# Graph attention and masked attention on one core: the product with the values between the next pair's scores

## The chip, the cores and the metric

The kernel runs on one core of a Trainium2 chip. The metric is the device time of one execution in microseconds (us); lower is better. Engines are named as in the profile: PE is TensorE, DVE is VectorE, ACT is ScalarE, POOL is GpSimd, and SP is the engine whose queue issues most transfers.

## The reference, cut to what matters

For each of 32 batches there are 512 rows of 512 numbers. Layer 0 is a graph attention, layer 1 a masked attention with 8 heads of 64; behind each stand a residual and a layer norm.

```python
# layer 0
h = X @ W                                             # 512 -> 256
e = leaky_relu(h @ a[0] + (h @ a[1]).T, 0.2)          # 512 x 512
alpha = softmax(e + NEG * (1 - adj), -1)
x1 = layernorm(x + concat([alpha @ h, h], -1))
# layer 1
q, k, v = (split_heads(x1 @ W.T + b) for W, b in ((Wq, bq), (Wk, bk), (Wv, bv)))
attn = softmax(where(adj == 0, -inf, (q @ k.T) / 8), -1)     # 8 heads of 512 x 512
out = layernorm(x1 + merge_heads(attn @ v) @ Wo.T + bo)
```

Everything is float32.

## The kernel before

All instructions are in program order on every engine: the text of the kernel is a schedule written out by hand, and each engine works through its own part of it without overtaking. The outer loop runs over batches `b`, the inner one over the four pairs of heads `hp`. While batch `b` is in its attention, the output product of batch `b-1` is finished (`finish_seven`, a generator that is advanced piece by piece with `next(seven)`), and layer 0 of `b+1` and the first products of `b+2` are done.

One pair goes like this:

- `head_scores(b, hp, i)`, called for tiles i = 0 to 3: PE makes the scores of 128 rows for both heads into PSUM (tile `ps`, four banks, so two tiles i at a time). DVE adds the mask and takes the maximum (`minus_max`, L315); ACT takes the exponential and its sum (L710) into a tile `p`.
- `head_blocks` (L722): DVE turns each of the eight `p` in blocks of 32 x 32 into the tile `t` (L330, eight instructions), inverts the sums (L717), sends them to memory (`d_tot`, L719), and SP issues 16 transfers of 128 KB from `t` to `pt` (`move_pair`, L347), which finish the transposition. `t` and `pt` have one buffer each: the first transposition of the next pair cannot begin until all 16 transfers of this one have landed.
- `head_inverse` (L750): POOL reads the inverse sums back, broadcast over partitions.
- `head_values` (L753): PE multiplies `pt` with the values (`pav`), and DVE multiplies with the inverse sums (L771).

Two products of PE are spread over the pairs, and their PSUM tiles share four banks with `pav`: `project_two` (queries and keys, `pw`, L547) after pairs 1 and 3, `project_v` (values, `pv`, L623) in pair 0, the output product of the batch before (`pf`, L791) in pairs 1 and 2, layer 0's product with the values (`po`, L477) after pair 1, and its projection (`ph`, L264) in pair 3. Each of `project_two`, `project_v` and `finish_seven` follows a scheme with seven products of half size: a first product goes to a bank, ACT copies it (`p1`), and a later product is accumulated onto the same bank, so that PE cannot go on before ACT has copied.

The order of PE in a batch before the change is, pair by pair (01 and 23 are the score tiles of the pair, and `pav` belongs to the pair before):

```
pair 0:  ps01, pv, ps23, pav, pv
pair 1:  ps01, pf, ps23, pav, po, pw
pair 2:  ps01, pf, ps23, pav, pf
pair 3:  ps01, ph, ps23, pav, pw
```

ACT's order matters too. In pair 1 the root for layer 0's norm (`ln_root` in `l0_output`, L286), which needs the statistics that DVE takes from all four `po`, stands ahead of the copies of `pw` (L571). In pair 3 the root for the norm of the finished batch (`ln_root`, after `out_stats`) stands ahead of the exponentials of tiles 2 and 3, and `out_norm` (L902) between these and the copies of `pw`.

Of the kernel before, what the change touches and what calls it, by code (L numbers as in the profile page):

```python
# [14 lines left out]
P = 128  # L15
# [11 lines left out]
def kernel(  # L27
# [47 lines left out]
    nc = tc.nc  # L75
    B, N, F = x.shape
# [65 lines left out]
            nc.sync.dma_start(xt_sb, src)  # L142
        st["xt", b] = xt_sb

    def load_x(b):
        x_sb = io.tile([P, NB, F], F32, name=f"x_{b}", tag="x", bufs=3)
        nc.sync.dma_start(x_sb, x[b].rearrange("(c p) f -> p c f", p=P))
        st["x1", b] = x_sb


# [175 lines left out]
    def transpose_blocks(t, i, src):  # L326

        nc.vector.transpose(  # L330
            t[:, :, :, i, :].rearrange("p r c q -> p c r q"),
            src.rearrange("p (c r k) -> p c r k", r=4, k=G),
        )
# [9 lines left out]
    def move_pair(dst, t):  # L343

        for g in range(4):
            for r in range(4):
                nc.sync.dma_start(  # L347
                    dst[r * G : (r + 1) * G, g], t[g * G : (g + 1) * G, r]
                )
# [119 lines left out]
            nc.vector.tensor_tensor(et[:, j, :], et[:, j, :], row, ALU.subtract)  # L469
            nc.scalar.activation(et[:, j, :], et[:, j, :], AF.Exp)  # L470

    def l0_values(b, i):
        h_sb, z = st["h", b], st["x1", b]
        et = st["et", b]
        po = (psum_s if b == 0 else psum)(f"po_{b}_{i}")[:, : F1 + 1]
        for j in range(NB):
            nc.tensor.matmul(  # L477
                po,
                et[:, j, i * P : (i + 1) * P],
                h_sb[:, j, 2:],  # L480
                start=(j == 0),
                stop=(j == NB - 1),
            )
        inv = small.tile([P, 1], F32, name=f"inv0_{b}_{i}", tag="inv0", bufs=2)
        nc.vector.reciprocal(inv, po[:, F1:])
        nc.vector.scalar_tensor_tensor(
            z[:, i, :F1], po[:, :F1], inv, z[:, i, :F1], ALU.mult, ALU.add
        )
# [126 lines left out]
    def project_v(b):  # L615

        x1t, tx = st["x1t", b], st["tx", b]
        half = F // 2

        def product(ps, columns, weights, start=True):  # L620
            for k in range(2):
                for c in range(FC // 2):
                    nc.tensor.matmul(  # L623
                        ps[:, k * half : (k + 1) * half],
                        columns(k, c),
                        weights(c),
                        start=start and k == 0 and c == 0,
                        stop=c == FC // 2 - 1,
                        skip_group_check=True,
                    )  # L630

        def a_(i, f):
            cols = slice(i * half, (i + 1) * half)
            return lambda c: wv_sb[:, 2 * f + c, cols]

        def s_(i):
            return lambda c: wvx_sb[:, i, c, :]

        def b_(f, j):
            return lambda k, c: x1t[:, 2 * j + k, 2 * f + c, :]  # L640

        def t_(i):
            return lambda k, c: tx[:, i, k, c, :]

        def copy(ps, name):
            t = prob.tile([P, N], F32, name=f"{name}_{b}_v", tag="p", bufs=PB)
            nc.scalar.copy(t, ps)
            return t

        out = []  # L650
        for j in range(2):
            v = act.tile([P, 2, F], F32, name=f"v_{b}_{j}", tag="v", bufs=2)
            st["v", b, j] = v
            out.append(v)

        def result(i, j, ps, other):
            nc.vector.tensor_tensor(
                out[j][:, :, i * half : (i + 1) * half],
                ps.rearrange("p (k d) -> p k d", k=2),
                other.rearrange("p (k d) -> p k d", k=2),  # L660
                ALU.add,
            )

        b1 = psum(f"pv1_{b}")
        product(b1, b_(0, 0), a_(0, 0))
        p1 = copy(b1, "p1")
        yield
        b3, b4 = psum(f"pv3_{b}"), psum(f"pv4_{b}")
        product(b3, t_(0), s_(0))
        p5 = copy(b3, "p5")  # L670
        product(b4, t_(2), a_(1, 0))
        p7 = copy(b4, "p7")
        nc.gpsimd.tensor_tensor(p7, p7, p5, ALU.add)
        product(b1, t_(1), s_(1), start=False)
        u2 = copy(b1, "u2")
        b2 = psum(f"pv2_{b}")
        product(b2, b_(1, 0), a_(0, 1))
        product(b3, b_(1, 1), s_(2), start=False)
        product(b4, t_(3), a_(1, 1), start=False)
        yield  # L680
        result(0, 0, b2, p1)
        result(0, 1, b3, u2)
        result(1, 1, b1, p7)
        result(1, 0, b4, u2)

    def head_scores(b, hp, i):
# [18 lines left out]
        for j in range(2):  # L705
# [6 lines left out]
            )  # L712
            st.setdefault(("p", b, hp), []).append((j, i, p))

    def head_sums(b, hp):
        total = st.pop(("tot", b, hp))
        nc.vector.reciprocal(total, total)  # L717
        d = dram.tile([2, P, NB], F32, name=f"d_tot_{b}_{hp}", tag="dtot")
        nc.sync.dma_start(d.rearrange("j p i -> p j i"), total)  # L719
        st["inv", b, hp] = d  # L720

    def head_blocks(b, hp):  # L722
        t = st.pop(("t", b, hp))
        for j, i, p in st.pop(("p", b, hp)):
            transpose_blocks(t[:, :, j], i, p)
        head_sums(b, hp)
        pt = prob.tile([P, 4, 2, FC, NB, G], F32, name=f"pt_{b}_{hp}", tag="pt", bufs=1)
        move_pair(pt, t)
        st["pt", b, hp] = pt

    def head_turn(b, hp):

        pt = prob.tile([P, 4, 2, FC, NB, G], F32, name=f"pt_{b}_{hp}", tag="pt", bufs=1)
        for k, (j, i, p) in enumerate(st.pop(("p", b, hp))):
            ps = psum_s(f"pt_{b}_{hp}_{i}_{j}")
            for c in range(FC):
                cols = slice(c * P, (c + 1) * P)
                nc.tensor.transpose(ps[:, cols], p[:, cols], ident)  # L738
            (nc.vector.tensor_copy if k % 2 == 0 else nc.scalar.copy)(
                pt[:, :, j, :, i, :].rearrange("p g c q -> p c g q"),  # L740
                ps.rearrange("p (c g q) -> p c g q", c=FC, g=4),
            )
        head_sums(b, hp)
        st["pt", b, hp] = pt

# [4 lines left out]
            nc.gpsimd.dma_start(inv[j * D : (j + 1) * D], d[j].partition_broadcast(D))  # L750
        st["inv", b, hp] = inv

    def head_values(b, hp, bank=None):  # L753
        pt, inv = st.pop(("pt", b, hp)), st.pop(("inv", b, hp))
        po = (bank or psum)(f"pav_{b}_{hp}")
        for c in range(NB):
            for j in range(2):
                head = 2 * hp + j
                nc.tensor.matmul(  # L759
                    po[j * D : (j + 1) * D, :],  # L760
                    st["v", b, c // 2][:, c % 2, head * D : (head + 1) * D],
                    pt[:, :, j, c, :, :].rearrange("p g i q -> p g (i q)"),
                    start=(c == 0),
                    stop=(c == NB - 1),
                )
        if hp % 2 == 0:
            st["ot", b, hp // 2] = act.tile(
                [P, 2, N], F32, name=f"ot_{b}_{hp // 2}", tag="ot", bufs=3
            )
        ot = st["ot", b, hp // 2][:, hp % 2]  # L770
        nc.vector.tensor_tensor(  # L771
            ot.rearrange("p (g i q) -> p g i q", g=4, i=NB),
            po.rearrange("p (g i q) -> p g i q", g=4, i=NB),
            inv.rearrange("p (g q) i -> p g i q", g=4),
            ALU.mult,
        )

    def finish_seven(b):


        z = st["x1", b]
# [44 lines left out]
        to = prob.tile([P, 2, N], F32, name=f"to_{b}", tag="rows", bufs=1)  # L826
        t1, t2, t3, t4 = b12, b22, to[:, :, : 2 * P], b21
        nc.gpsimd.tensor_tensor(t3, b22, b12, ALU.subtract)
        nc.gpsimd.tensor_tensor(t1, b12, b11, ALU.subtract)
        nc.gpsimd.tensor_tensor(t2, b22, t1, ALU.subtract)  # L830
        nc.gpsimd.tensor_tensor(t4, t2, b21, ALU.subtract)
# [4 lines left out]
        add(nc.vector, 0, 0, b1)  # L836
        yield
        b4, b5 = psum(f"pf4_{b}"), psum(f"pf5_{b}")
        product(b1, t2, s_(1), start=False)
        u2 = copy(b1, "u2")  # L840
        product(b4, t3, a_(1, 0))
        p7 = copy(b4, "p7")
        add(nc.gpsimd, 0, 1, u2)
        add(nc.gpsimd, 1, 0, u2)
        yield
        product(b5, t1, s_(0))
        product(b4, t4, a_(1, 1), start=False)
        yield
        add(nc.vector, 1, 1, b5)
# [125 lines left out]
    def output_bias():  # L975
# [4 lines left out]
        )  # L980
        nc.vector.tensor_tensor(bo_sb, pb, bo_sb, ALU.add)

    before = None
    turned = {(0, 2), (B - 2, 2), (B - 1, 2), (B - 1, 3)}
    for b in range(B):
        more = b < B - 1
        seven = finish_seven(b - 1) if b > 0 else None
        for hp in range(NP):
# [44 lines left out]
                out_norm(b - 1)  # L1033
            if (b, hp) not in turned:
                head_blocks(b, hp)
            if hp == 0 and b > 0 and more:
                load_x(b + 1)
            if before is not None:
# [45 lines left out]
            else:  # L1084
# [14 lines left out]
                head_inverse(b, 3)  # L1099
                if b == 0:  # L1100
                    weight_negative(OUTPUT)
                    add_bias(1)
            before = (b, hp)
    b = B - 1
    ln_root(f"1_{b - 1}")
# [72 lines left out]
```

## Time and profile before

| what | value |
|---|---|
| median of 3 runs | 3072.32 us (3070.25 to 3075.42) |
| profiled execution | 3078.44 us, span 3076.7 us |
| PE busy | 3044.9 us, 99% of the span |
| DVE busy | 2493.5 us, 81% |
| ACT busy | 1536.4 us, 50% |
| POOL busy | 1254.5 us, 41% |
| transfers `pt<-t` | 1984 of 128 KB, issued by SP |

Busy time is what an engine's instructions took; the chain is the work that ended last, followed back to its start. A line such as L330 is a line of the kernel before. In a timeline the columns are the start, the duration (from the start of the first to the end of the last of merged instructions), the engine, the line, the operation, output and inputs, and a count; square brackets give the engine's idle time ahead of it and what ended it.

### The profile page before, as it was taken

What the parts mean: (1) busy time and instruction counts of PE and PEld (TensorE: products, weight loads), DVE (VectorE), ACT (ScalarE), POOL (GpSimd) and SP (SyncE); (2) the same over time, 40 slices, a digit from 0 to 9 for tenths busy, and PEclk for the clock granted to TensorE, in tenths of its full rate; (3) what the DMA queues carried; (4) which work ended last, traced back from release to release, by engine and by line L of the source; (5) the groups of instructions that cost most, each with busy time, mean ns of one, the idle gap of its engine ahead of it and who ended that gap; (6) DMA issues with size and microseconds to landing.
All of it is one profiled execution on the core that took longest, in us unless ns stands there. A gap on an engine that the chain in (4) does not pass through costs nothing.

```text
span 3076.7 us, 44833 instructions
## 1 busy us (share of the span) xinstructions
PE 3044.9 (99%) x13492; PEld 2064.9 (67%) x13492; DVE 2493.5 (81%) x5707; ACT 1536.4 (50%) x3264; POOL 1254.5 (41%) x1224
## 2 busy tenths in 40 slices
PE   8999999999999999999999999999999999999999
PEld 6666666666666666666666666666666666666665
DVE  7788788888888888888888888878888877888765
ACT  4445554545544455544455444555454554445544
POOL 4343444444344434344443444343444434443422
PEclk9999999999999999999999999999999999999999
DMA  6456665566566656655665656566556656666642
GB/s 185 113 134 155 153 159 146 150 162 165 145 156 150 161 154 154 162 146 147 163 163 145 154 151 163 154 151 163 149 146 162 164 144 157 151 160 155 155 102 66
DMA packets 244865, 462.54 MB, mean 150 GB/s; under 512 B 94544, under 2 KB 97104, under 8 KB 244624
## 3 DMA queue, kind: packets, MB, share of 16 engines
q1 hardware_dynamic: 232160, 425.83, 54.9%
q0 software_dynamic: 12464, 33.84, 4.2%
q8 instruction: 109, 1.79, 0.3%
q14 instruction: 132, 1.08, 0.1%
HBM read 132.65 MB, written 34.27 MB: 54 GB/s over the span
## 4 chain that ended last, share of the span: by engine, by line
PE 90%; DVE 3%; SPq 2%; issue 1%; POOL 1%; DMA 1%; ACT 1%; DVEq 0%; ACTq 0%; POOLq 0%
PE pw L547 23%; PE ps L701 14%; PE pav L759 14%; PE pv L623 12%; PE pf L791 12%; PE po L477 7%; PE ph L264 7%; SPq L347 2%; DVE t L330 1%; DMA d_least<-least 1%; DVE p L315 1%; PE pf L863 0%; PE pt L738 0%; DVE junk L315 0%; DMA adjs_sb<-in_adj_dram 0%
## 5 line engine op out<-in xcount | busy, mean ns | idle before, releaser
L710 ACT ACTIVATE p<-p,least 128x512 f32<-128x512 f32 x1024 | 725.8, 711 | 518.5 <-DVE least L315 315.6
L315 DVE CUSTOM_DVE_ANT_0 p<-ps,mask 128x512 f32<-128x512 f32 x1024 | 645.0, 686 | 224.0 <-PE ps L701 223.9
L330 DVE STREAM_TRANSPOSE t<-p 128x512 f32<-128x512 f32 x992 | 603.0, 675 | 8.7 <-issue 6.5
L701 PE MATMUL ps<-qk 64*128 64x512 f32 x2048 | 512.5, 617 | 4.1 <-DVE qk L584 3.8
L759 PE MATMUL pav<-pt,v 128*64 128x512 f32 x2048 | 467.7, 598 | 7.7 <-DMA pt<-t 4.0
L759 PEld LDWEIGHTS pav<-pt,v 128*64 128x64 f32 x2048 | 138.9, 136 | 322.0 <-issue 283.0
L701 PEld LDWEIGHTS ps<-qk 64*128 64x128 f32 x2048 | 179.2, 186 | 210.7 <-issue 163.6
L459 POOL TENSOR_TENSOR et<-et,mask0t 128x512 f32<-128x512 f32 x126 | 144.4, 1159 | 341.6 <-ACT et L455 341.4
L750 POOL DMA_DIRECT2D inv<-d_tot x256 | 134.4, 530 | 276.9 <-DMA d_tot<-tot 92.8
L814 POOL TENSOR_TENSOR x<-x,u_o 128x512 f32<-128x512 f32 x93 | 117.0, 1272 | 306.8 <-ACT u_o L809 275.4
L477 PE MATMUL po<-h,et 128*128 128x257 f32 x1024 | 233.9, 387 | 2.8 <-ACT et L470 2.2
L264 PE MATMUL ph<-w_sb,xt 128*128 128x258 f32 x1024 | 233.4, 385 | 0.3 <-DVE w_sb L190 0.3
L477 PEld LDWEIGHTS po<-h,et 128*128 128x128 f32 x1024 | 190.4, 191 | 58.9 <-POOL x L379 25.3
L264 PEld LDWEIGHTS ph<-w_sb,xt 128*128 128x128 f32 x1024 | 192.2, 190 | 50.8 <-PE ps L701 22.0
L379 POOL TENSOR_TENSOR x<-x,h 128x256 f32<-128x256 f32 x128 | 85.6, 701 | 306.7 <-DMA x<-in_x_dram 306.7
L536 POOL TENSOR_TENSOR x<-x,bo_sb 128x512 f32<-128x512 f32 x128 | 158.5, 1272 | 94.1 <-DVE x1t_b L330 94.1
L710 ACT ACTIVATION_READ_ACCUMULATOR p<-p,least 128x1 f32 x1024 | 192.1, 188 | 0.0
L710 ACT ACT_TABLE_LOAD x62 | 79.5, 1283 | 218.9 <-DVE least L315 218.4
L286 ACT ACTIVATE rstd<-mv,eps 128x4 f32<-128x4 f32 (+1 forms) x66 | 19.6, 297 | 335.3 <-DVE mv L281 331.9
L280 DVE BATCH_NORM_STATS2 stats<-x 128x6 f32<-128x512 f32 x252 | 171.8, 682 | 16.2 <-POOL x L814 3.1
L791 PE MATMUL pf<-wo_sb,ot 128*128 128x256 f32 x744 | 182.2, 388 | 0.0
L791 PE MATMUL pf<-wox_sb,ot 128*128 128x256 f32 x744 | 179.0, 383 | 0.0
(154 smaller groups left out, 5453.0 us busy)
## 6 DMA issues: line engine op xcount, KB each, us to landing
pt<-t SPq DMA_DIRECT2D x1984, 128.0 KB, 3.5
x<-in_x_dram SPq DMA_DIRECT2D x32, 1024.0 KB, 5.4
inv<-d_tot POOLq DMA_DIRECT2D x256, 128.0 KB, 3.9
xt<-in_xt_dram SPq DMA_DIRECT2D x31, 1024.0 KB, 5.6
x1t<-x1t_b SPq DMA_DIRECT2D x496, 64.0 KB, 2.0
out_dram<-x SPq DMA_DIRECT2D x31, 1024.0 KB, 5.7
rows<-d_att SPq DMA_DIRECT2D x31, 512.0 KB, 3.7
rows<-d_least SPq DMA_DIRECT2D x31, 256.0 KB, 3.6
```

Of the source, the lines that this page charges most:

```text
L264: nc.tensor.matmul(ps, lhs(c), rhs(c), start=(c == 0), stop=(c == FC - 1))
L280: nc.vector.bn_stats(stats, z[:, i, :])
L315: nc.vector.tensor_tensor_reduce(out=out, in0=scores, in1=mask, scale=-1.0, scalar=MIN_INIT, op0=ALU.add, op1=ALU.min, accum_out=least,)
L330: nc.vector.transpose(t[:, :, :, i, :].rearrange("p r c q -> p c r q"), src.rearrange("p (c r k) -> p c r k", r=4, k=G),)
L477: nc.tensor.matmul(po, et[:, j, i * P : (i + 1) * P], h_sb[:, j, 2:], start=(j == 0), stop=(j == NB - 1),)
L536: nc.gpsimd.tensor_tensor(z[:, i, :], z[:, i, :], bo_sb, ALU.add)
L547: nc.tensor.matmul(ps[:, k * half : (k + 1) * half], weights(k, c), moving(c), start=start and k == 0 and c == 0, stop=c == FC // 2 - 1, s ...
L623: nc.tensor.matmul(ps[:, k * half : (k + 1) * half], columns(k, c), weights(c), start=start and k == 0 and c == 0, stop=c == FC // 2 - 1, ...
L701: nc.tensor.matmul(ps, qk[rows, 0, i * P : (i + 1) * P], qk[rows, 1, :], start=True, stop=True)
L710: nc.scalar.activation(p, p, AF.Exp, bias=least, scale=-1.0, accum_out=total[:, j, i : i + 1])
L759: nc.tensor.matmul(po[j * D : (j + 1) * D, :], st["v", b, c // 2][:, c % 2, head * D : (head + 1) * D], pt[:, :, j, c, :, :].rearrange("p ...
L791: nc.tensor.matmul(ps[:, k * half : (k + 1) * half], columns[:, c, k * P : (k + 1) * P], weights(c), start=start and k == 0 and c == 0, st ...
```

## The change

For batches 1 to 29 a new function `middle_batch` writes out the order of a batch; batches 0, 30 and 31 keep the old loop. In the middle batches:

- In pairs 0, 1 and 2 the product `pav` of the pair before (`head_products`) is issued between score tiles 01 and 23; in pair 3 it stays behind tile 3. The division by the sums (`head_divide`) stays behind the pair's transpositions.
- Four of the eight transpositions of a pair are issued after the maxima of tiles 0 and 1 (`head_blocks` is called twice), the other four after tiles 2 and 3. The move to `pt` comes ahead of the write of the inverse sums.
- `project_v` runs wholly after pair 0's scores. The first two pieces of `finish_seven` go to the end of pair 0, and the tile `po` 0 follows them there; the other three `po` stay after pair 1. The four sums on POOL move to the middle of pair 1, the product b1 to the end of pair 2's scores, and the rest stays behind pair 2.
- The load of `x` for the next batch is issued by POOL, between two of these sums, and not by SP.

In all batches `project_v` writes its (1, 1) result first, and `finish_seven` does two products ahead of the accumulation onto b1. `add_bias(1)` moves from the end of batch 0 to batch 1.

```diff
-    def load_x(b):
+    def load_x(b, engine=nc.sync):
...
-        nc.sync.dma_start(x_sb, x[b].rearrange("(c p) f -> p c f", p=P))
+        engine.dma_start(x_sb, x[b].rearrange("(c p) f -> p c f", p=P))
...
     def head_blocks(b, hp):
-        t = st.pop(("t", b, hp))
         for j, i, p in st.pop(("p", b, hp)):
-            transpose_blocks(t[:, :, j], i, p)
-        head_sums(b, hp)
+            transpose_blocks(st["t", b, hp][:, :, j], i, p)
+
+    def head_move(b, hp):
         pt = prob.tile([P, 4, 2, FC, NB, G], F32, name=f"pt_{b}_{hp}", tag="pt", bufs=1)
-        move_pair(pt, t)
+        move_pair(pt, st.pop(("t", b, hp)))
...
         nc.gpsimd.tensor_tensor(t3, b22, b12, ALU.subtract)
+        if between:
+            between()
         nc.gpsimd.tensor_tensor(t1, b12, b11, ALU.subtract)
...
         b4, b5 = psum(f"pf4_{b}"), psum(f"pf5_{b}")
+        product(b4, t3, a_(1, 0))
+        p7 = copy(b4, "p7")
+        product(b5, t1, s_(0))
         product(b1, t2, s_(1), start=False)
         u2 = copy(b1, "u2")
-        product(b4, t3, a_(1, 0))
-        p7 = copy(b4, "p7")
...
+    def pair_ends(b, hp):
+        head_blocks(b, hp)
+        head_reciprocal(b, hp)
+        head_move(b, hp)
+        head_sums(b, hp)
+
+    def middle_batch(b):
+        seven = finish_seven(b - 1, lambda: load_x(b + 1, nc.gpsimd))
+        for hp in range(NP):
+            last = (b, hp - 1) if hp > 0 else (b - 1, NP - 1)
+            head_scores(b, hp, 0)
+            head_scores(b, hp, 1)
+            if hp < 3:
+                head_products(*last)
+            if hp == 0:
+                l0_scores(b + 1, [0, 1])
+            elif hp == 1:
+                next(seven)
+                l0_add_h(b + 1)
+            elif hp == 2:
+                add_bias(b + 1)
+            head_blocks(b, hp)
+            if hp == 3:
+                out_stats(b - 1)
+                for i in range(NB):
+                    l0_project(b + 2, i)
+                l0_columns(b + 2)
+                ln_root(f"1_{b - 1}")
+            head_scores(b, hp, 2)
+            head_scores(b, hp, 3)
+            if hp == 2:
+                next(seven)
+            elif hp == 3:
+                out_norm(b - 1)
+                head_products(*last)
+            pair_ends(b, hp)
+            if hp == 2:
+                next(seven)
+            head_divide(*last)
+            if hp == 0:
+                l0_row(b + 1)
+                l0_scores(b + 1, [2, 3])
+                leaky(st["row", b + 1])
+                values = project_v(b)
+                next(values)
+                next(values)
+                l0_weights(b + 1)
+                head_inverse(b, 0)
+                steps(values)
+                next(seven)
+                next(seven)
+                l0_value_product(b + 1, 0)
+            elif hp == 1:
+                l0_output(b + 1)
+                load_xt(b + 2)
+                two = project_two(b, 1)
+                next(two)
+                l0_norm(b + 1)
+                next(two)
+                head_inverse(b, 1)
+                blocks = x1_blocks(b + 1)
+                for part in (blocks, two, blocks, two, blocks):
+                    next(part, None)
+            elif hp == 2:
+                steps(seven)
+                x1_sums(b + 1, nc.gpsimd)
+                head_inverse(b, 2)
...
+            else:
+                l0_maxima(b + 2)
+                l0_write(b + 2)
+                l0_read(b + 2)
+                store(b - 1)
+                steps(project_two(b + 1, 0))
+                head_inverse(b, 3)
...
     for b in range(B):
+        if 0 < b < B - 2:
+            middle_batch(b)
+            before = (b, NP - 1)
+            continue
```

More of the change, by code (lines that the diff above doesn't have):

```diff
@@ L470, in l0_weights, with l0_value_product @@
             nc.scalar.activation(et[:, j, :], et[:, j, :], AF.Exp)
-    def l0_values(b, i):
-        h_sb, z = st["h", b], st["x1", b]
-        et = st["et", b]
+    def l0_value_product(b, i):
+        h_sb, et = st["h", b], st["et", b]
         po = (psum_s if b == 0 else psum)(f"po_{b}_{i}")[:, : F1 + 1]
@@ L483, in l0_values @@
             )
+        st["po", b, i] = po
+    def l0_values(b, i):
+        z = st["x1", b]
+        if ("po", b, i) not in st:
+            l0_value_product(b, i)
+        po = st.pop(("po", b, i))
         inv = small.tile([P, 1], F32, name=f"inv0_{b}_{i}", tag="inv0", bufs=2)
@@ L680, in project_v @@
         yield
+        result(1, 1, b1, p7)
         result(0, 0, b2, p1)
         result(0, 1, b3, u2)
-        result(1, 1, b1, p7)
         result(1, 0, b4, u2)
@@ L713, in head_scores, with head_reciprocal @@
             st.setdefault(("p", b, hp), []).append((j, i, p))
+    def head_reciprocal(b, hp):
+        total = st["tot", b, hp]
+        nc.vector.reciprocal(total, total)
     def head_sums(b, hp):
         total = st.pop(("tot", b, hp))
-        nc.vector.reciprocal(total, total)
         d = dram.tile([2, P, NB], F32, name=f"d_tot_{b}_{hp}", tag="dtot")
@@ L751, in head_inverse, with head_products @@
         st["inv", b, hp] = inv
-    def head_values(b, hp, bank=None):
-        pt, inv = st.pop(("pt", b, hp)), st.pop(("inv", b, hp))
-        po = (bank or psum)(f"pav_{b}_{hp}")
+    def head_products(b, hp, bank=None):
+        pt = st.pop(("pt", b, hp))
+        po = st["pav", b, hp] = (bank or psum)(f"pav_{b}_{hp}")
         for c in range(NB):
@@ L765, in head_values, with head_divide @@
                 )
+    def head_divide(b, hp):
+        po, inv = st.pop(("pav", b, hp)), st.pop(("inv", b, hp))
         if hp % 2 == 0:
@@ L776, in head_values, with finish_seven @@
         )
-    def finish_seven(b):
+    def head_values(b, hp, bank=None):
+        head_products(b, hp, bank)
+        head_divide(b, hp)
+    def finish_seven(b, between=None):
         z = st["x1", b]
@@ L845, in finish_seven @@
         yield
-        product(b5, t1, s_(0))
         product(b4, t4, a_(1, 1), start=False)
@@ L981, in output_bias @@
         nc.vector.tensor_tensor(bo_sb, pb, bo_sb, ALU.add)
+    def pair_ends(b, hp):
+        head_blocks(b, hp)
+        head_reciprocal(b, hp)
+        head_move(b, hp)
[61 more added lines that the diff above has]
+                head_inverse(b, 2)
+                if b == 1:
+                    add_bias(1)
+            else:
[5 more added lines that the diff above has]
+                head_inverse(b, 3)
@@ L1035 @@
                 head_blocks(b, hp)
+                head_reciprocal(b, hp)
+                head_sums(b, hp)
+                head_move(b, hp)
             if hp == 0 and b > 0 and more:
@@ L1101 @@
                     weight_negative(OUTPUT)
-                    add_bias(1)
             before = (b, hp)
```

## The prediction

> **What bounds the kernel now.** I read the page first: is one engine always at work?
>
> ```profile
> PE 3044.9 (99%) x13492; PEld 2064.9 (67%) x13492; DVE 2493.5 (81%) x5707; ACT 1536.4 (50%) x3264; POOL 1254.5 (41%) x1224
> ...
> pt<-t SPq DMA_DIRECT2D x1984, 128.0 KB, 3.5
> ```
>
> A busy PE might still be a slow PE, so I took one batch by windows:
>
> ```profile
> 1518.00:1612.00 94.00, 94.00 (x419) 63.86 (x418) 77.58 (x178) 47.56 (x101) 39.53 (x38) 1.00 0.62 160
> ```
>
> PE has no gap at all in 94 us and its clock is 1.00. In the timeline eight records of 256 columns that follow their like take 1.725 us; a batch has 416 records of that weight, 89.8 us, and the rest up to the period of 93.83 is spread over 20 switches between full products, `ps` and `pav`: about 0.2 us each. So PE sets the time, at a floor. The waits of PE say where that floor is thin:
>
> ```profile
> PE pav L759 <- DMA pt<-t: 4.0, 2, 2.8
> PE pav L759 <- DMA d_least<-least: 2.7, 6, 1.4
> ```
>
> `pav` is the only product that ever waits in the middle: the one of pair 3, in pair 0 of the next batch. The move to `pt` lands just in time there. On the chain the `pw` of pair 1 starts at 379.27 and, 22 batches on, at 2447.06: 93.99 a batch.
>
> Next, how close the others follow. Pair 1, PE, then ACT:
>
> ```profile
> 1587.94 1.99 PE L701 MATMUL ps<-qk 64*128 64x512 f32 x8
> 1589.85 3.65 PE L759 MATMUL pav<-pt,v 128*64 128x512 f32 x16
> 1593.44 7.25 PE L477 MATMUL po<-h,et 128*128 128x257 f32 x32
> ...
> 1604.84 1.03 PE L547 MATMUL pw<-tx,wk_sb 128*128 128x256 f32 x4
> 1605.84 1.13 PE L547 MATMUL pw<-tx,wqx_sb 128*128 128x256 f32 x4
> ```
>
> ```profile
> 1605.02 0.30 ACT L286 ACTIVATE rstd<-mv,eps 128x4 f32<-128x4 f32 x1 [10.89 <-DVE mv L281]
> 1605.22 1.54 ACT L571 COPY p<-pw 128x512 f32<-128x512 f32 x3
> ```
>
> PE's step from 1604.84 to 1605.84 is 1.00 where its neighbours take 0.86: the accumulation at 1605.84 waited 0.1 us for ACT's copy, which waited for the root, which waited for DVE. There is no slack here at all.
>
> Pair 3, DVE, SP and ACT (`ps` of tiles 2 and 3 begins at 1544.68):
>
> ```profile
> 1548.87 4.86 DVE L330 STREAM_TRANSPOSE t<-p 128x512 f32<-128x512 f32 x8 [0.21 <-issue]
> ```
>
> ```profile
> 1532.67 11.09 SPq L347 DMA_DIRECT2D pt<-t  x16
> ...
> 1554.46 10.51 SPq L347 DMA_DIRECT2D pt<-t  x16
> ```
>
> ```profile
> 1551.16 2.92 ACT L902 ACTIVATE x<-x,shift,rstd 128x512 f32<-128x512 f32 x4
> 1553.98 1.04 ACT L571 COPY p<-pw 128x512 f32<-128x512 f32 x2
> ```
>
> One move keeps SP for 10.0 to 11.1 us and its last transfer lands 2.5 to 3.6 us after its issue, so `t` is taken for 13.1 us from the last transposition on (0.15 + 9.9 + 3.0 without the write of the sums ahead of it). Before, the next transpositions came 16.8 us later.
>
> **The change, part by part.** All times in us; "ps23" is the start of tiles 2 and 3.
>
> *Switches of PE.* With `pav` between `ps01` and `ps23`, and `pv` no longer split, pairs 0, 1 and 2 have four switches, not five: 3 x 0.19 = 0.57 a batch, 16.5 in 29 batches. Nothing else of PE's work goes; this is all that can be won. The trace has no switch from `pav` to `ps`; its bounds are 0 and 0.4, the nearest row is `ps` to `pav` (1.91 against 1.92 to a full product), so I take 0.19.
>
> *Pair 0.* ACT does the exponentials (first one 1.95 after ps23, four end at 4.8), then two masks' inputs of layer 0 (2.36), then `p1` (0.59): the copy is done at 7.75. Before, a `pav` of 3.58 lay in between on PE. Now PE has 1.92 + 1.83 + 2 x 1.725 = 7.2 and then waits: **0.65**. From ps23 of pair 0 to that of pair 1: 7.85 + 4 x 1.725 (rest of `pv`) + 3.45 (`pf`) + 1.8 (`po` 0) + 5.5 (`ps01`, `pav`) = 25.55.
>
> *Pair 1.* DVE: maxima end at 1.16 + 2.45, four transpositions 2.45, sums and division 1.0, then `l0_output` 6.45 (1598.53 to 1604.98): the statistics are done at 13.5. ACT needs 0.9 for root and copy: 14.4. PE has 1.92 + 5.4 (three `po`) + 5.2 (three `pw`) = 12.6. Before, both stood at 17.9: DVE has lost 3.5 (four transpositions, two additions of `pf`), PE has lost 5.4 (`pav`, one `po`). The wait is **1.85**. ps23 to ps23: 14.45 + 6.9 + 0.1 + 5.5 = 26.95.
>
> *Pair 2.* The transpositions of x1 end 16.35 after the start of `l0_output` (from 1598.53 to 1521.05 of the batch before plus 93.83), so DVE is free 23.45 after pair 1's ps23, does maxima, half the transpositions, maxima and the other half (4 x 2.45) and ends at 33.3. SP sends x1 first (16 issues, 10.24, until 33.85), then the move. It lands at 33.9 + 12.9 = 46.8, which is 19.85 after pair 2's ps23. The new order in `finish_seven` gives the addition of b1 on DVE (done at 7.1) just time: no wait of PE, where the old order would cost some 3.4.
>
> *Pair 3.* PE reaches `ps01` 10.8 after pair 2's ps23, DVE could transpose at 14.5, but `t` is free at 19.85. Behind the waiting transpositions stand, on DVE, the statistics of the finished batch and the maxima of tiles 2 and 3; behind these ACT's root, exponentials, `out_norm` and copies; behind these PE. Transpositions 19.9 to 22.35, statistics (3.2) 25.55, root to first exponential 1.6 (1546.71 to 1548.32), exponentials 2.85, `out_norm` 2.82, copy 0.6: 33.45. PE, after `ph`, ps23 at 19.9, `pav` and three `pw`, is at 30.65: wait **2.9**. (Before, the copy was 0.95 early.)
>
> *Pair 0 of the next batch.* The last exponential of pair 3 is at 30.05, the last transposition ends at 30.75, the move lands 13.1 later at 43.85. PE is through `pw` at 40.5 and `ps01` at 42.4, where `pav` now stands: wait **1.5**. Before, `pav` came 3.84 later and still met the landing.
>
> Period: 43.9 (ps23 of pair 2 to this `pav`) + 3.58 + 25.55 + 26.95 = 100.0; against 93.99 that is +6.0 a batch, 29 x 6.0 = **+174**.
>
> *At nothing:* the load of x on POOL. POOL's issues of 4 to 256 KB take 0.53 to 0.76; x has four times the rows of the largest, so 0.55 to 2.2, and lands by 30 after ps23 of pair 0; the statistics that need it begin at 33.5. POOL itself waits until 18.9 in `head_inverse`, since the sums are now written behind the move, and the four sums of `finish_seven`, 5.1, and `l0_add_h`, 2.7, stand behind that; cover about 3, beyond which each us is one us of PE. SP is relieved of 0.58. The (1, 1) result first, `add_bias(1)` moved, and batches 0, 30, 31: POOL and DVE have gaps there; at most a few us in all, either way.
>
> **Two rules of the Trainium skill.** "DMA: Bandwidth & Descriptors", section "Issuing engines are not separate DMA queues", says that the sequencer's time to start a transfer is usually small beside the transfer. Then `t` would be free some 4 after the last transposition (landing 3.5 on the page), pair 3 and the `pav` behind it would not wait, and the sum is 29 x (0.65 + 1.85 - 0.57) = 56, 3128. The row says 10.0 to 11.1 of issue for a move; I take the row.
>
> "TensorE: Matmul & The Clock Gate", section "What's actually happening", says that the array falls to half clock after an idle window of about 3.4 us. No wait above is that long: by the rule, nothing. This trace is stricter:
>
> ```profile
> 75.86 8.97 PE L477 MATMUL po<-h,et 128*128 128x257 f32 x32 [2.21 <-ACT et L470]
> ```
>
> ```profile
> 76.00:79.50 3.50, 3.50 (x10) 2.60 (x11) 3.42 (x12) 3.50 (x9) 0.00 (x0) 0.57 0.91 221
> ```
>
> A pause of 2.21 was followed by 3.4 us at half clock, and 32 records took 8.97 for 7.25: 1.7. A pause of 1.49 at 37.55 was not. So the wait of 2.9 in pair 3 may cost 1.7 more, 49 in all. In the middle I take 0, because the `pav` that waits 1.5 next is bound by the move and takes up such a loss; 49 goes to the upper end.
>
> **The rivals.** *Hidden better.* If DVE gets through pair 3 without the wait for `t` (transfers land sooner, or the statistics' lateness is absorbed), there remain 0.65 + 1.85 + some 0.5 at `pav`: +2.5 to 4.5 a batch, 3145 to 3203. For it: landings vary from 2.2 to 4.8. Against: 16 issues never took under 10.
>
> *Half clock, or x late.* +7.7 a batch: 3295 to 3345.
>
> *Faster.* Only the switches count and every wait is covered: 3072.3 - 16.5 = 3056. It decides from the point where ACT's copy in pair 1 is done by 12.6 (1.85 sooner) and the move of pair 2 frees `t` by 14.5, that is in 8 us and not 13.1. No row shows either; only a wrong reading of the order on ACT or of `t`'s one buffer would.
>
> *It does not do what it says:* the move could wait for the write of the sums after all; 0.6 more, inside the range.
>
> **How the numbers follow.** The profiled execution took 3078.44, 6 above the median of 3072.32; its own sum would be 3252, on the median's footing 3246. The waits as worked out, with 0.5 either way for each landing: 0.62 (3205 to 3295). Hidden better: 0.19. Half clock or x late: 0.12. Faster: 0.05. Within 0.2% (about 6 us, what a measurement of this kernel can tell): 0.02. The range of 3160 to 3315 takes in most of the second case and the near half of the third. So faster 0.05, same 0.02, slower 0.93.
>
> **What would show it.** Right: PE busy at about 94% of the span; waits of PE on ACT's copies in `pw` (L547), near 4 to 5 a batch, and on transfers at `pav`, near 1.5; DVE's transpositions `t` waiting for `pt<-t` some 5 us a batch; the maxima of pair 3's tiles 2 and 3 starting 5 to 6 after their scores. A period near 100.0. Wrong: transpositions that don't wait, or PE above 98%.

## The result

The changed kernel takes 3242.03 us (median of 5 runs, 3236.07 to 3245.05) against 3073.44 of the kernel before in the same runs: ratio 1.0546, 95% interval 1.0531 to 1.0562, so 5.5% slower. The forecast was 3246. The profiled execution took 3240.09, its span 3238.3.

From the profile of the changed kernel: busy times, and the chain by engine.

```profile
PE 3067.0 (95%) x13492; PEld 2074.7 (64%) x13492; DVE 2537.0 (78%) x5707; ACT 1535.6 (47%) x3264; POOL 1284.2 (40%) x1253
...
PE 51%; DVE 20%; SPq 10%; ACT 8%; DMA 4%; issue 4%; POOL 1%; DVEq 0%; ACTq 0%; POOLq 0%
```

PE does the same 13492 products, but is idle for 171.3 us of the span (3238.3 - 3067.0) where it was idle for 31.8; the other 22 of the 162 us by which the span grew are in PE's busy time. The chain, 90% PE before, is half on other engines. What PE waits for (the engine and product that wait, what ended the wait; total, times, longest):

```profile
PE pw L553 <- ACT p L577: 67.2, 30, 3.3
PE po L476 <- DVE inv L491: 45.9, 29, 1.6
PE pav L769 <- DMA d_least<-least: 13.8, 12, 2.4
PE pv L629 <- ACT p_v L653: 9.1, 30, 0.3
```

Each of these comes once or less per middle batch, and each belongs to one pair. Pair 3, by DVE, ACT and PE (`ps` of tiles 2 and 3 begins at 1522.31):

```profile
1521.65 2.49 DVE L330 STREAM_TRANSPOSE t<-p 128x512 f32<-128x512 f32 x4 [3.70 <-DMA d_tot<-tot]
```

```profile
1531.80 2.91 ACT L921 ACTIVATE x<-x,shift,rstd 128x512 f32<-128x512 f32 x4
1534.62 1.52 ACT L577 COPY p<-pw 128x512 f32<-128x512 f32 x3
```

```profile
1535.32 1.10 PE L553 MATMUL pw<-tx,wqx_sb 128*128 128x256 f32 x4 [2.07 <-ACT p L577]
...
1546.10 3.65 PE L769 MATMUL pav<-pt,v 128*64 128x512 f32 x16 [1.71 <-DMA d_tot<-tot]
```

DVE's first four transpositions wait for `t`, and all that stands behind them on DVE is late. So ACT's copy comes 12.3 after `ps`, where it came 9.3 after it in the kernel before, and PE waits for the copy. The move that starts late in turn holds `pav` in pair 0. Pair 1, on PE and then on DVE:

```profile
1575.14 1.99 PE L707 MATMUL ps<-qk 64*128 64x512 f32 x8
1577.06 3.74 PE L476 MATMUL po<-h,et 128*128 128x257 f32 x16
1582.38 1.98 PE L476 MATMUL po<-h,et 128*128 128x257 f32 x8 [1.58 <-DVE inv L491]
...
1589.45 1.13 PE L553 MATMUL pw<-tx,wqx_sb 128*128 128x256 f32 x4
```

```profile
1581.24 0.99 DVE L784 TENSOR_TENSOR ot<-pav,inv 128x512 f32<-128x512 f32 x1
1582.15 0.16 DVE L491 RECIPROCAL inv<-po 128x1 f32<-128x1 f32 x1
1582.35 0.48 DVE L492 SCALAR_TENSOR_TENSOR x<-po,inv,x 128x256 f32<-128x256 f32 x1
```

The accumulation at 1589.45 stands 14.3 after `ps`, as worked out, but nearly all of the time was lost ahead of it: `po` tile 3 had waited for a bank of PSUM. When it starts at 1582.38, DVE has ended the division of `pav` at 1582.23 and is still reading `po` tile 0, until 1582.83. So tile 3 takes over the bank of `pav`, and PE comes to it before the division is done, because tile 0 no longer stands ahead of it in pair 1.

### The profile page after: what moved, and what is told of

Read it like the earlier page. It is cut to its first block, busy times and chain, and to the rows that moved or that the text cites. A ratio compares the mean times of both kernels' runs of the same rounds, so it can differ in the third digit from the quotient of the medians.

```text
span 3238.3 us, 44630 instructions
## 1 busy us (share of the span) xinstructions
PE 3067.0 (95%) x13492; PEld 2074.7 (64%) x13492; DVE 2537.0 (78%) x5707; ACT 1535.6 (47%) x3264; POOL 1284.2 (40%) x1253
## 4 chain that ended last, share of the span: by engine, by line
PE 51%; DVE 20%; SPq 10%; ACT 8%; DMA 4%; issue 4%; POOL 1%; DVEq 0%; ACTq 0%; POOLq 0%
PE pw L553 15%; SPq L347 10%; PE pav L769 9%; PE ps L707 7%; DVE t L330 7%; PE pv L629 7%; PE pf L808 7%; DVE p L315 6%; ACT p L716 4%; PE po L476 4%; DVE stats L280 2%; ACT et L455 2%; DMA d_tot<-tot 1%; PE ph L264 1%; DMA xt<-in_xt_dram 1%
## 5 line engine op out<-in xcount | busy, mean ns | idle before, releaser
L330 DVE STREAM_TRANSPOSE t<-p 128x512 f32<-128x512 f32 x992 | 629.5, 684 | 124.8 <-DMA d_tot<-tot 75.0
L476 PE MATMUL po<-h,et 128*128 128x257 f32 x1024 | 244.9, 388 | 48.5 <-DVE inv L491 45.9
L606 POOL TENSOR_TENSOR p<-p,p 128x512 f32<-128x512 f32 x64 | 83.9, 1310 | 473.4 <-ACT p L577 473.4
L831 DVE TENSOR_TENSOR x<-x,pf 128x512 f32<-128x512 f32 x186 | 125.4, 677 | 150.9 <-POOL x L831 90.7
L459 POOL TENSOR_TENSOR et<-et,mask0t 128x512 f32<-128x512 f32 x126 | 156.4, 1257 | 144.6 <-ACT et L455 144.6
L553 PE MATMUL pw<-tx,wqx_sb 128*128 128x256 f32 x512 | 139.1, 394 | 67.2 <-ACT p L577 67.2
```

Source lines behind the costliest of these rows:

```text
L330: nc.vector.transpose(t[:, :, :, i, :].rearrange("p r c q -> p c r q"), src.rearrange("p (c r k) -> p c r k", r=4, k=G),)
L476: nc.tensor.matmul(po, et[:, j, i * P : (i + 1) * P], h_sb[:, j, 2:], start=(j == 0), stop=(j == NB - 1),)
L553: nc.tensor.matmul(ps[:, k * half : (k + 1) * half], weights(k, c), moving(c), start=start and k == 0 and c == 0, stop=c == FC // 2 - 1, s ...
L831: engine.tensor_tensor(to, to, term.rearrange("p (k d) -> p k d", k=2), ALU.add)
```

## The experiments

All times are compared by their ratio to the kernel before in the same runs, with the 95% interval in brackets; one hundredth is 30.8 us. The changed kernel stands at 1.0546.

**po tile 0 back in pair 1.**

```diff
                 next(seven)
                 next(seven)
-                l0_value_product(b + 1, 0)
```

> One part undone: the tile po 0 goes back from the end of pair 0 to pair 1, where the other three stand. Theory of the prediction: PE's work between the scores of pair 1 and the accumulation onto b1 was 1.8 us too short for DVE and ACT, so a tile there costs nothing and in pair 0 it costs its whole 1.8 us. The changed kernel's wait of 1.58 us at po tile 3 goes, none takes its place at the copy of pw, and pav of pair 0 still finds its pt. 29 x 1.75 = 51 us less: 3191 (3180 to 3205). Rival: pair 1 is set by the chain on DVE from the pair before, wherever the tile stands: 3235 to 3245.

Measured: 3200.43, ratio 1.0398 (1.0379 to 1.0418), 46 us less than the changed kernel. The 45.9 us of waits at `po` are gone from the list and no wait took their place in pair 1: PE now comes to tile 3 only when the division has freed the bank. The moved tile cost nearly its own length: it filled time that pair 0 did not have free, and left pair 1 short. What falls short of the expected 51 may be the clock: in the profiled run, the slowest of the four, it is 0.986 where the changed kernel has 0.994. No run takes the two apart.

**Pair 3 whole.**

```diff
-            head_blocks(b, hp)
+            if hp < 3:
+                head_blocks(b, hp)
```

> One part undone in one pair: in pair 3 the first four transpositions are not issued behind the first maxima, all eight come behind tiles 2 and 3. Theory: DVE waits there for t (3.7 us), and statistics, maxima, ACT's root, exponentials and copies stand behind it; without it the wait of PE at pw in pair 3 (2.1 us) goes, while the move starts with eight transpositions behind the scores, so that pav of pair 3 waits 2.3 and not 1.7: 1.5 us a batch, 43 less, 3199 (3180 to 3215). Rival: ACT is late in pair 3 for its own order (root, table load, out_norm), not for t; then the wait at pw stays and the later move adds 2.4 at pav: 3290 to 3310.

Measured: 3200.56, ratio 1.0396 (1.0380 to 1.0411), 46 us less. The waits at `pw` fall from 67.2 us to 3.6, and those at `pav` rise from some 28 to some 66, as the theory has it (2.3 a batch). So ACT was late for `t`, not for its own order.

```profile
PE pw L553 <- ACT p L577: 3.6, 3, 3.1
```

**pav of pair 3 behind the scores of pair 0.**

```diff
-            if hp < 3:
+            if hp in (1, 2):
                 head_products(*last)
...
+            if hp == 0:
+                head_products(*last)
             pair_ends(b, hp)
```

> One part undone in one pair: in pair 0 the product pav of the batch before's pair 3 stands behind score tiles 2 and 3, as in the kernel before; in pairs 1 and 2 it stays between. Theory: its wait (1.7 us) is the move landing late, 1.92 us of scores ahead of it cover it, and one switch of 0.2 goes: 1.7 to 1.95 a batch, 49 to 56 less, 3190 (3180 to 3200). Rival: the landing is not what bounds a batch, PE would be late by as much at the copies of pv or at pair 1: 3235 to 3245.

Measured: 3223.95, ratio 1.0471 (1.0456 to 1.0487), 23 us less: half of what was expected. Two reasons show. The expectation took 1.7 a batch from one batch; over the middle batches the wait at `pav` is near 0.9 (some 25 us in 24 waits). And the four score tiles in a row wait inside the merged record, 4.87 where two times 1.92 would be 3.84; over the middle batches this is about 1 us each time. The four banks of `ps` hold two tiles, so the second two wait until DVE has read the first two.

```profile
1533.37 4.87 PE L707 MATMUL ps<-qk 64*128 64x512 f32 x16
```

**Half of pair 2's transfers on POOL.** (The new argument of `move_pair` and `head_move` is left out here.)

```diff
         for g in range(4):
             for r in range(4):
-                nc.sync.dma_start(
+                (nc.sync, second)[r % 2].dma_start(
...
-        head_move(b, hp)
+        head_move(b, hp, nc.gpsimd if hp == 2 else nc.sync)
```

> One suspected cost taken away: eight of the 16 transfers of pair 2's move from t to pt are issued by POOL and eight by SP; everything else as in the changed kernel. Theory: SP's issue (0.64 us each) sets how long t is taken; the last landing comes about 5 us sooner, DVE's transpositions in pair 3 don't wait, and neither do pw in pair 3 (2.1) nor most of pav behind it (1.7): 3.6 us a batch, 104 less, 3138 (3125 to 3165). Rival: the 16 transfers are bound by the DMA engines that carry them: landing as late as before, 3235 to 3250.

Measured: 3229.36, ratio 1.0497 (1.0479 to 1.0514), only 15 us less. It lies between the two expectations, and far nearer to the rival's. SP's and POOL's issues, then DVE's next transposition:

```profile
1499.06 9.64 SPq L347 DMA_DIRECT2D pt<-t  x8
```

```profile
1499.28 3.92 POOL L347 DMA_DIRECT2D pt<-t  x8 [8.08 <-issue]
```

```profile
1511.29 2.49 DVE L330 STREAM_TRANSPOSE t<-p 128x512 f32<-128x512 f32 x4 [2.41 <-DMA d_tot<-tot]
```

Then the middle of the move, here and in the changed kernel (start and end; length; busy time of PE, PEld, DVE, ACT and POOL; PE's clock; busy share of the DMA engines; GB/s):

```profile
1503.30:1508.70 5.40, 5.40 (x25) 3.71 (x26) 3.64 (x9) 1.57 (x5) 5.32 (x5) 1.00 0.94 214
```

```profile
1511.50:1519.40 7.90, 7.90 (x37) 5.64 (x36) 3.82 (x10) 3.78 (x11) 7.02 (x6) 1.00 0.92 205
```

POOL has issued its eight in 3.9, but SP now takes 9.64 for eight, and `t` is free 12.2 after the first issue; in the changed kernel, with 16 on SP, it was 12.3 (1509.35 to 1521.65). Over the middle batches it is free 12.5 after the last transposition, in the changed kernel 13.0: half a microsecond is won, not five. The DMA engines are 94% busy at 214 GB/s, and with SP alone they were already 92% busy at 205. At these rates the two MB of a move take about 10 us, whoever issues them.

**pav between the scores, alone, in the kernel before.** (`head_products` is the first half of `head_values`, as in the changed kernel.)

```diff
...
             head_scores(b, hp, 0)
             head_scores(b, hp, 1)
+            if hp < 3 and 0 < b < B - 2:
+                head_products(*before)
```

> One part alone in the kernel before: in batches 1 to 29 the product pav stands between score tiles 01 and 23 in pairs 0, 1 and 2; transpositions, po, project_v and finish_seven stay as before. Theory: pav was the cover behind the second scores. Pair 1 waits for the copy of pw by the 3.6 us that pav took there; pair 0 meets pt 3.84 us before it lands; pair 2 waits some 2.3 us for the addition of b1. 9.7 us a batch, 280 in all, about 3355 against 3078 (3290 to 3390), worse than the whole change. Rival: the early pav itself is harmless and the halves or the moved po do the damage: 3070 to 3120.

Measured: 3716.80, ratio 1.2064 (1.2018 to 1.2109), 635 us more than before. The direction holds and the rival falls, but the loss is more than twice what was expected. PE's waits in one batch, without those below 0.6:

```profile
1506.18 3.59 PE L796 MATMUL pf<-wox_sb,ot 128*128 128x256 f32 x8 [2.45 <-DVE x L819]
...
1546.83 5.35 PE L759 MATMUL pav<-pt,v 128*64 128x512 f32 x16 [3.09 <-DMA d_least<-least]
...
1563.66 3.34 PE L623 MATMUL pv<-wv_sb,x1t 128*128 128x256 f32 x8 [2.26 <-DVE ot L776]
...
1576.64 5.35 PE L759 MATMUL pav<-pt,v 128*64 128x512 f32 x16 [3.96 <-DVE et L469]
...
1596.29 2.00 PE L477 MATMUL po<-h,et 128*128 128x257 f32 x8 [2.57 <-DVE ot L776]
```

The addition of b1 (2.45, expected 2.3) and `pt` in pair 0 (3.09, expected 3.84) are as worked out. The wait for the copy of `pw` in pair 1, expected at 3.6, did not come: PE waits 1.1 us for it in the whole run. Not foreseen were three things. In pair 1 `pav` stands too early as well: it starts at 1576.64, when the last transfer of pair 0's move has landed at 1576.18 (the DVE instruction named had nothing to do with it). The bank of `pav` is held by an early product until a division that comes late (2.26 at `pv`, 2.57 at `po`). And the clock: four of these five waits are followed by records at half speed (3.59 for 1.99, 5.35 for 3.65). The mean granted clock is 0.944 against 0.998, which in 3717 us is worth up to 200 us. The other parts of the change cover much of what the early `pav` lays open: with them it costs 169, without them 635.

**The halves alone, in the kernel before.** (`head_half` does the transpositions of the tiles made so far; `head_blocks` does the rest.)

```diff
...
             head_scores(b, hp, 0)
             head_scores(b, hp, 1)
+            if 0 < b < B - 2:
+                head_half(b, hp)
```

> The other part alone in the kernel before: in batches 1 to 29 four of a pair's eight transpositions stand behind the maxima of tiles 0 and 1; pav and all else stay as before. Theory: in pairs 3 and 0 DVE waits for t (4 to 5 us and 2 us), the maxima of tiles 2 and 3 are late by it, and in pair 3 ACT's root and exponentials too; PE waits 2.5 to 4 us a batch: 3150 to 3195. Rival: the halves cost nothing where pav stays behind, since pav covers 3.6 us: 3070 to 3085.

Measured: 3309.45, ratio 1.0755 (1.0734 to 1.0775), 232 us more, above the 72 to 117 that was expected. The waits are of the kind named:

```profile
1556.14 2.49 DVE L330 STREAM_TRANSPOSE t<-p 128x512 f32<-128x512 f32 x4 [6.32 <-ACT att L387]
```

```profile
PE pw L547 <- ACT p L571: 99.8, 30, 4.0
PE po L477 <- DVE x L817: 43.2, 29, 1.7
```

In pair 3 DVE stands still for 6.3 (the ACT instruction named had long been done; what was awaited is `t`), and PE waits 3.3 a batch for the copy. Missing from the expectation were 1.5 a batch at `po`, ended by an addition on DVE, and a clock of 0.982 against 0.998, worth up to 53 us.

**Pairs 0 and 3 in the old order, 1 and 2 in the new one.** Against the changed kernel:

```diff
-            if hp < 3:
+            if hp in (1, 2):
                 head_products(*last)
             if hp == 0:
+                values = project_v(b)
+                next(values)
                 l0_scores(b + 1, [0, 1])
...
-            head_blocks(b, hp)
+            if hp in (1, 2):
+                head_blocks(b, hp)
...
+            if hp in (0, 3):
                 head_products(*last)
...
-                values = project_v(b)
-                next(values)
                 next(values)
                 l0_weights(b + 1)
...
-                l0_value_product(b + 1, 0)
```

> A version put together from what the runs showed: pairs 0 and 3 in the order of the kernel before (project_v begun between the scores, pav behind tile 3, all eight transpositions at the end), pairs 1 and 2 in the new order, po 0 back in pair 1. Theory: of the changed kernel's waits only 0.2 to 0.3 us a batch are left, and two switches of 0.19 are saved: 93.7 a batch against 93.99, 3 to 9 us less than the kernel before: ratio 0.997 to 0.999. Rival: what one wait gives up another takes (pav of pair 0 at its edge, the copy of pw in pair 1): ratio 1.003 to 1.015.

Measured: 3072.47 against 3078.54, ratio 0.9982 (0.9975 to 0.9990): 0.18% faster than the kernel before, with 1 outside the interval. No wait of PE in the middle batches is left in the list but some tenths at `pav`. The chain shows one thing still: 40 records of `pf` in pair 2 take 9.04 from start to start, where 0.2157 each and the switches make 8.8.

**The addition of b1 first.** Against the version above:

```diff
+            if hp == 2:
+                next(seven)
             pair_ends(b, hp)
-            if hp == 2:
-                next(seven)
```

> The version of pairs 0 and 3 in the old order and pairs 1 and 2 in the new one, with one more edit: in pair 2 DVE adds the product b1 to x ahead of the second four transpositions, not behind them. Theory: the 16 records of pf around the accumulation onto b1 take 3.67 from start to start where 3.45 is the work; the addition is late by 0.22, done ahead it is early, and the later move has room, since pair 3 transposes only at its end. 0.22 a batch, 6 us less: ratio to the kernel before 0.9955 to 0.997. Rival: the transpositions and the move pass their 0.6 us on to pav of pair 2 or to pair 3: ratio 0.998 or above.

Measured: 3066.57 against 3080.99, ratio 0.9956 (0.9943 to 0.9970). The chain, first of the version above, then of this one:

```profile
1517.91 9.04 PE pf L808 x40
```

```profile
1513.55 8.83 PE pf L808 x40
```

A wait of 0.21 had stood within the busy time, where no list of waits shows it. On the chain the `pw` of pair 3 starts at 225.54 and, 14 batches on, at 1536.97: 93.67 a batch, against 93.99 in the kernel before.

## Why the prediction was right, point by point

The mechanism held: `t` is busy until the move of pair 2 has landed, and DVE, ACT, PE and the next move are late in turn; pair 1 is too short on PE. That 3246 and 3242 lie within 4 us of each other is in part luck, since several terms were off and the errors went both ways.

- **Period.** Worked out: 100.0 a batch. On the chain, `pw` starts at 389.67 and 22 batches on at 2577.22: 99.4. The four waits less the switches (0.65 + 1.85 + 2.9 + 1.5 - 0.57) make 6.3, while the walk through the batch made 6.0; the prediction used the second and did not notice the difference. The runs have 5.4: the waits were smaller than worked out, by 1.4 from start to start, and two terms taken as nothing, the clock and a wait in pair 2, gave about 0.6 back.
- **How a wait is read.** The list of waits is short by a little, because a record of PE reaches past the start of the next one. At the `pw` in pair 3 the list has 2.07, but from 1532.23 to 1535.32 is 3.09, where four records take 0.86: 2.23 were lost. Figures "from start to start" are of this kind, as means over the middle batches.
- **Switches, 0.57 won.** Held: from `pav` to `ps` takes 3.58 (1546.10 to 1549.68), as from `pav` to a full product. The two last versions, which keep two of the three savings, are faster than before.
- **Pair 0, 0.65.** Direction right; 0.3 in the list, 0.47 from start to start. PE came when it was worked out (1555.15 and 1.725 for the last eight records, 7.2 after `ps`), and the copy let it go on at 7.67 (1549.68 to 1557.35), 0.18 sooner than worked out.
- **Pair 1, 1.85.** The total is right (14.3 from `ps` to the accumulation, 14.45 worked out), the place is not: 1.58 of it, 1.7 from start to start, is the wait of `po` tile 3 for the bank of `pav`, which the prediction did not look at. Only 0.1 is left for the copy. The size does not depend on it, since the copy would have held PE until 14.3 in any case. With the tile back both waits are gone.
- **Pair 2, no wait.** 0.2 within the busy time, shown by the last version.
- **Pair 3, 2.9; `pav` behind it, 1.5.** 67.2 in 30 waits makes 2.2 (2.35 from start to start), and `pav` about 0.9. The term that was mis-sized is the landing. In pair 2 `t` was to be free 13.5 after the last transposition, and DVE goes on after 13.0 in the mean; in pair 3 the move was to land 13.1 after it, and lands after 12.3 (11.9 to 13.4). In the batch shown `t` was free 19.4 after pair 2's `ps` (1502.26 to 1521.65), not 19.85. That the wait for `t` causes the wait at `pw` was shown by pair 3 whole.
- **The signs named.** PE is busy for 95% (94 named). The waits for ACT's copies at `pw` come to 2.2 a batch (4 to 5 named), since those of pair 1 stand at `po`. In pair 3 DVE waits 3.7 a batch for `t` (some 5 named), since it comes there 1.2 later than worked out and `t` is free 0.5 sooner, and the maxima of tiles 2 and 3 start 4.9 after `ps` (5 to 6 named).
- **The rule on issuing.** The 10 us of a move were right as a measured length. The reason given for them, SP's own time, was wrong: with half of the issues on POOL the move was hardly shorter. The rule of "DMA: Bandwidth & Descriptors", section "Issuing engines are not separate DMA queues", that issuing on several engines saves only the sequencer's time fits that run. The prediction drew 3128 from it by taking the transfers themselves for short; the DMA engines' 92% say that they are not.
- **The clock.** Taken as 0, with 1.7 a batch at the upper end. In the changed kernel it is between: mean clock 0.994 against 0.998, some 14 us in all (the stretches at half clock lose 22 us, 8 in the kernel before). It falls in few batches after pauses like those of all the others:

```profile
639.06 1.16 PE L553 MATMUL pw<-tx,wqx_sb 128*128 128x256 f32 x4 [2.24 <-ACT p L577]
640.02 1.91 PE L553 MATMUL pw<-tx,wkx_sb 128*128 128x256 f32 x4
```

The four records at 640.02 take 1.91 where 1.03 is usual. A pause of 2.07 at 1535.32 had no such effect. "TensorE: Matmul & The Clock Gate", section "What's actually happening", says that the window of activity runs free. The traces agree: in the changed kernel all stretches at half clock but the last are 3.41 long, and each begins a whole number of 3.413 after the first. So the time can be divided into windows of that grid (start and end; length; PE busy; clock; DMA share; GB/s):

```profile
636.56:639.97 3.41, 1.17 (x6) 1.00 0.52 115
639.97:643.38 3.41, 3.41 (x9) 0.50 0.89 198
1530.85:1534.27 3.42, 2.40 (x12) 1.00 0.01 2
1534.27:1537.68 3.41, 2.36 (x11) 1.00 0.92 203
```

The pause that cost the clock fell into one window and left PE idle for 2.24 of it; the other was cut by the border, 1.02 and 1.05. So a window need not be idle as a whole, as the prediction had read the rule; 2.24 of 3.41 were enough. The run with `pav` alone has 111 such stretches: of its windows at full clock, those in which PE was idle for 2.02 or more were all followed by half clock, and those with 2.00 or less never. In the changed kernel the two kinds overlap a little (half clock after 1.72 to 2.93, none after up to 1.91).

- **POOL at nothing.** The load of x took 0.78 on POOL (0.55 to 2.2 had been bounded), and the first addition of h was over before DVE asked for it. Not tested alone.

The 22 us by which PE's busy time grew are a balance: the switches took some 16 away (29 x 0.57), the clock added some 14, and the ends of records that reach into a pause some 16. About 8 us stay open.

## What to carry to other kernels

When one engine works without a gap, moving its work can win no more than its own overheads. Work that is moved forward can uncover the waits behind it, and each must be worked out along the queue of the engine that answers (here DVE, then ACT, then the move). With one buffer for a transfer of 12 us, an early start of the next one wins nothing unless as much other work lies between. Parts of such a change can be taken apart: the new order in pairs 1 and 2 alone, with one tile put back and one addition moved, is 0.44% faster than the kernel before, and with pairs 0 and 3 and that tile it is 5.5% slower.

## What the runs showed of the hardware that was not expected

- An SP issue stretches when the DMA engines are full: 1.2 us each (9.64 for 8) in place of 0.63 (10.05 for 16), with POOL issuing beside it. So the length of an issue in the profile is not SP's own time alone. The move of x1, with half the bytes, takes 0.68 an issue (10.82 for 16) at a DMA share of 0.47, so there the engines were not full; what bounds it no run here shows.
- Whether a pause of PE costs the clock depends on a grid: a little over 2 us of idle time within one window of 3.413 us was followed by half clock for the next window, the same pause across a border was not. Many such pauses, as with `pav` alone, made this up to a third of the loss (200 of 635 us); few, as in the changed kernel, a twelfth.
